# A state-space block and linear attention on one core: the C product moved behind the second scan at slot 10, and half of the gate's Silu read out of PSUM

## The chip, the cores and the metric

The kernel runs on one core of a Trainium2 chip. A core has five engines that run side by side and wait for each other by semaphores: TensorE (PE in the profile) multiplies matrices into PSUM, VectorE (DVE) and GpSimd (POOL) work elementwise, ScalarE (ACT) evaluates functions such as Exp and Silu, and SyncE (SP) issues most of the transfers. Each engine works its own instructions off in order. The metric is the device time of one execution in microseconds; of several executions the median is taken.

## The reference

The input `x` has 4 images of 512 channels with 64 x 64 places, so 4 sequences of 4096 places. Layer 0 takes a group norm, then a layer norm, cuts the channels into 4 chunks of 128 and sends each through a Mamba block. Layer 1 is a linear attention of 8 heads. Each layer is added to its input. Of the Mamba block, what matters here is:

```python
xz = jnp.einsum('bld,ed->ble', x, in_proj_w)
xi, z = jnp.split(xz, 2, axis=-1)
...
xc = jax.nn.silu(xc + conv_b[None, :, None]).transpose(0, 2, 1)
...
def step(h, inp):
    dt_t, B_t, C_t, x_t = inp
    dA = jnp.exp(dt_t[:, :, None] * A)
    h = dA * h + (dt_t * x_t)[:, :, None] * B_t[:, None, :]
    y = jnp.einsum('bds,bs->bd', h, C_t)
    return (h, y)
...
y = ys.transpose(1, 0, 2) + xc * D_param
y = y * jax.nn.silu(z)
return jnp.einsum('bld,od->blo', y, out_proj_w)
```

There are 256 inner channels and 16 states a channel. Two things of this are touched by the change: the product of the state `h` with `C`, and the Silu of `xc` and of the gate `z`.

## The kernel before

**Tiling.** A step is one image, one tile of 512 places and one chunk of 128 channels: 4 x 8 x 4 = 128 steps, the chunk innermost. The 256 inner channels are two halves `e` of 128. For the recurrence, 32 channels with 4 states each fill the 128 partitions; one scan instruction (line 739) runs 512 places of such a row block. A step has 16 slots (line 674) of two scans each, so 32 scans. Slots 0 to 7 belong to half 0, slots 8 to 15 to half 1. Two slots share one `h` buffer (of two, line 733), one row block of `B` and one of `C`.

**A slot** (function `slot`, line 725) issues in this order: GpSimd's product `bx` for the slot after next (`drive`, line 721, three buffers); the loads of later `B` and `C` rows; then twice a scan and, right after it, the Exp that makes the decay for the third scan ahead (`decay`, line 713, three PSUM banks, `LEAD` on line 53). In an even slot the product of the two slots before with `C` comes between the two scans: `product` (line 759) is one VectorE instruction over 4 x 384 places; the last 128 places of each row are multiplied on GpSimd (line 751), with a `C` that a transfer brings (`c_sb`). After `product` comes `fold_states` (line 761), all on TensorE: the next `C` rows into PSUM (line 765, one bank, which the product has to leave first), for the first group of a half the term with `D_param` (the four matmuls of `diagonal`, line 768), and four matmuls that sum over the states into `y` (line 771). The fold is the last reader of `h` and so frees its buffer, which is written again two slots later.

**What is put beside it.** At the end of each slot `after` (line 1108) issues the work of the slot: first what was put off for it (`later`, line 75), then fixed work by slot number, then pieces of norms, projections and attention as TensorE has room for them. The inputs of the step after next are made this way (`inputs`, line 579): at slot 9 the matmul of the gate branch's second half is issued into a bank of a ring of three (`work_bank`, line 67), and at slot 10 the copy out of it (line 608) into `xz`. At slot 10 also stands `silu` (lines 1047 and 1147): one ScalarE instruction over all of `xz`, 4 x 512 places: `xc` of both halves, then `z` of both. Silu and Exp lie in different table sets of ScalarE, so a table load stands before Silu and another after it (line 1149). Slots 3 (softplus, with loads too) and 10 are `AWAY` (line 675); long VectorE instructions of the norms are put there. At slot 9 GpSimd multiplies the gate of half 0 (line 781), and at slot 4 it makes dt times x (line 628). From slot 12 on the matmuls on `xz` for B, C and dt follow (`mixers`, line 642).

The order of all this in the main loop is written by hand; nothing is planned at compile time, and the two steps before the loop run `silu` alone. The lines that set the place of the product are

```python
            if i == 0 and jj == 0 and g:
                product(g - 1)
                fold_states(g - 1, last)
```

where `i` is the scan within the slot and `jj` is 0 in even slots.

Of the kernel before, what the change touches and what calls it, by code (L numbers as in the profile page):

```python
# [10 lines left out]
AF = mybir.ActivationFunctionType  # L11
# [13 lines left out]
def kernel(  # L25
# [24 lines left out]
    nc = tc.nc  # L50
# [4 lines left out]
    NH = DI // P  # L55
# [23 lines left out]
    def work_bank(name, behind=1):  # L79
        held[0] += behind  # L80
        return ps_w.tile([P, T], F32, tag="w", name=name)
# [4 lines left out]
    def later(n, what):  # L86

        done = []

        def both():  # L90
            what()
            done.append(True)

        if now[0] is None:
            both()
        else:
            due.append((now[0] + n, both))
        return done
# [22 lines left out]
    def mm(out_, lhsT, rhs, abreast=1, **how):  # L121

        work["mm"] += (0.25 if rhs.dtype == BF16 else 1.0) * rhs.shape[-1] / T / abreast
        nc.tensor.matmul(out_, lhsT, rhs, **how)  # L124
# [250 lines left out]
    def bc(v, n):  # L375
        return v.unsqueeze(1).to_broadcast([P, n, v.shape[-1]])
# [202 lines left out]
    def inputs(f, xn, c, nm):  # L579

        xz = f["xz"] = wk.tile([P, 2, NH, T], F32, tag="xz", name=f"xz_{nm}", bufs=3)
        pc = [None] * NH

        def taps(e, ks):
            for k in ks:
                mm(
                    pc[e], w_cv[:, k, e * P : (e + 1) * P], xn[:, c, k : k + T],
                    start=(k == 0), stop=(k == NTAP - 1),
                )

        def take(e):
            nc.scalar.activation(xz[:, 0, e, :], pc[e], AF.Identity, bias=cb[:, e : e + 1])

        for e in range(NH):
            pc[e] = work_bank(f"pc_{nm}_{e}", 0)
            taps(e, range(NTAP // 2))
            yield
            taps(e, range(NTAP // 2, NTAP))
            later(1, lambda e=e: take(e))
            yield  # L600
        for e in range(NH):
            pz = work_bank(f"pz_{nm}_{e}", 0)
            mm(
                pz, w_z[:, e * P : (e + 1) * P], xn[:, c, NTAP - 1 : NTAP - 1 + T],
                start=True, stop=True,
            )

            later(1, lambda e=e, pz=pz: nc.scalar.copy(xz[:, 1, e, :], pz))  # L608
            yield

    def time_banks(f, nm):
# [62 lines left out]
    SLOTS = NH * NQ * JJ  # L674
    AWAY = (3, 10)

    def place(g):

        n, r = divmod(g, SLOTS)
        e, r = divmod(r, NQ * JJ)  # L680
        return n, e, *divmod(r, JJ)
# [10 lines left out]
    def b_row(g):  # L692
        n, e, q, _ = place(g)
        b_all[g // JJ] = wk.tile([P, T], F32, tag="b_all", name=f"b_all_{g}", bufs=3)
        for_states(b_all[g // JJ], fs[n]["b_rows"], q)

    def c_tail(g):
        n, e, q, _ = place(g)
        c_sb[g // JJ] = wk.tile([P, T - CUT], F32, tag="c_sb", name=f"c_sb_{g}", bufs=2)
        for_states(c_sb[g // JJ], fs[n]["c_rows"], q)  # L700
# [7 lines left out]
    def decay(k):  # L708

        n, e, q, jj = place(k // 2)  # L710
        j = jj * 2 + k % 2
        dAs[k] = ps_d.tile([P, T], F32, tag="dA", name=f"dA_{k}")
        nc.scalar.activation(  # L713
            dAs[k], fs[n]["d_all", e][:, 0, j, :], AF.Exp, scale=a_t[:, e, j, q : q + 1]
        )

    def drive(g):

        n, e, q, jj = place(g)
        bxs[g] = wk.tile([P, 2, T], F32, tag="bx", name=f"bx_{g}", bufs=3)  # L720
        nc.gpsimd.tensor_tensor(  # L721
            bxs[g], fs[n]["d_all", e][:, 1, jj * 2 : jj * 2 + 2, :], bc(b_all[g // JJ], 2), ALU.mult
        )

    def slot(g, last, after):
        n, e, q, jj = place(g)
        b, t, c = steps[n]
        if g + 2 < last:
            drive(g + 2)
        if jj == 0:  # L730
            if g + 3 * JJ < last:
                b_row(g + 3 * JJ)
            hs[g // JJ] = wk.tile([P, NJ, T], F32, tag="h", name=f"h_{g}", bufs=2)
        elif g + 1 < last:
            c_tail(g + 1)
        h = hs[g // JJ]
        for i in range(2):
            j = jj * 2 + i
            nc.vector.tensor_tensor_scan(  # L739
                h[:, j, :], dAs.pop(2 * g + i), bxs[g][:, i, :],  # L740
                0.0 if t == 0 else st[:, c, e, q, j : j + 1], ALU.mult, ALU.add,
            )
            if 2 * g + i + LEAD < 2 * last:
                decay(2 * g + i + LEAD)
            if i == 0 and jj == 0 and g:
                product(g - 1)
                fold_states(g - 1, last)
        del bxs[g]
        if jj == JJ - 1:
            nc.gpsimd.tensor_copy(st[:, c, e, q, :], h[:, :, T - 1])  # L750
            nc.gpsimd.tensor_tensor(  # L751
                h[:, :, CUT:], h[:, :, CUT:], bc(c_sb.pop(g // JJ), NJ), ALU.mult
            )
        after()

    def product(g):

        own = hs[g // JJ][:, :, :CUT]
        nc.vector.tensor_tensor(own, own, bc(c_all.pop(g // JJ), NJ), ALU.mult)  # L759

    def fold_states(g, last):

        n, e, q, _ = place(g)
        if g + 1 < last:
            c_row(g + 1)
        if q == 0:
            ys[n, e] = ps_y.tile([P, T], F32, tag="y", name=f"y_{n}_{e}")
            diagonal(ys[n, e], dg[:, e, :], fs[n]["xz"][:, 0, e, :])
        h = hs.pop(g // JJ)
        for j in range(NJ):  # L770
            mm(
                ys[n, e][j * BLK : (j + 1) * BLK, :], fold, h[:, j, :],
                start=False, stop=(q == NQ - 1), abreast=NJ,
            )
# [234 lines left out]
    fs = [{} for _ in steps]  # L1009
# [33 lines left out]
    def step_inputs(n):  # L1043
        b, t, c = steps[n]
        return inputs(fs[n], xn[b, t], c, names[n])

    def silu(n):
        nc.scalar.activation(fs[n]["xz"], fs[n]["xz"], AF.Silu)  # L1048

    ahead, late, rest, light = [], [], [], []  # L1050

# [19 lines left out]
    run(tile_norm(0, 0))  # L1071
    run(step_inputs(0))
    silu(0)
    run(mixers(fs[0], names[0]))
    b_row(0)
# [9 lines left out]
    for g in range(2):  # L1085
        drive(g)
    run(step_inputs(1))
    silu(1)
    run(mixers(fs[1], names[1]))
    nc.scalar.preload_act_table_set("natural_log_exp_and_others")  # L1090
# [3 lines left out]
    with tc.manual_schedule():  # L1094
        credit, seen, mix, held[0], held_x[0] = 0.0, work["mm"], iter(()), 0, 0
        for n, (b, t, c) in enumerate(steps):
            f, nm = fs[n], names[n]
# [9 lines left out]
            for s in range(SLOTS):  # L1107
                def after():
# [38 lines left out]
                    if s == 10 and n + 2 < N:  # L1147
                        silu(n + 2)
                        nc.scalar.preload_act_table_set("natural_log_exp_and_others")
# [21 lines left out]
                    seen = work["mm"]  # L1171

                slot(n * SLOTS + s, N * SLOTS, after)
            fs[n - 1].clear() if n else None
        product(N * SLOTS - 1)
# [64 lines left out]
```

## Time and profile before

| | |
|---|---|
| median of 3 runs | 7940.75 us (7933.85 to 7962.12) |
| profiled execution: time | 7963.09 us |
| profiled execution: span of the trace | 7961.4 us |
| granted TensorE clock, mean | 0.897 |
| first to last scan | 122.4 to 7493.4 us |
| product with C (L759) | 1024 times, mean 1726 ns |
| GpSimd's part of it (L751) | 1024 times, mean 1270 ns |
| copy of z out of PSUM (L608) | 256 times, mean 580 ns |
| Silu (L1048) | 128 times, mean 1911 ns |
| each table load | 1283 ns |

How to read the profile: the page of one execution gives each engine's busy time and its share of the span; then groups of equal instructions, with line, engine, operation and what they write and read, count, busy time and mean, and after a second bar the time in which the engine stood idle just before them and who ended most of it. The view of waits has who waited for whom, the total, the number of times and the longest. The timeline has start, length, engine, line, operation and count, and in brackets the idle time before it with its releaser. The profile names only one releaser for a wait that has several.

### The profile page before, as it was taken

The page shows a single profiled execution, that of the slowest core. Times are in us where ns is not written, and L with a number is a line of the kernel's source. Part 1 is how long each engine was busy: PE and PEld are TensorE (multiplying, and loading weights), DVE is VectorE, ACT ScalarE, POOL GpSimd, SP SyncE. Part 2 cuts the span into 40 slices and gives each one's busy share as a digit, 9 for nine tenths or more (in the row PEclk, how much of TensorE's full clock was granted, in tenths as well). Part 3 has the DMA queues.
Part 4 walks back from the last instruction along what each step waited for, and adds up shares of the span by engine and source line. Part 5 has one row for each costly group of instructions (what it writes and reads, how often), then busy time and mean ns, then how long its engine had stood idle before and what let it go on. Part 6 is the DMA issues. An engine that isn't in the chain of part 4 may idle for free.

```text
span 7961.4 us, 90563 instructions
## 1 busy us (share of the span) xinstructions
PE 6453.6 (81%) x24835; PEld 2120.0 (27%) x24880; DVE 6977.7 (88%) x5766; ACT 5507.6 (69%) x8321; POOL 6880.5 (86%) x4597
## 2 busy tenths in 40 slices
PE   5676777677789888888788888898688888888599
PEld 1121212112223222322222223332122332322144
DVE  5999999999999999989999999998999999988600
ACT  4667777777777777767777777677777777777421
POOL 4999999999999899989999899898999999889600
PEclk7888888888899999998899999899899999999799
DMA  5666666666666666777766666677666666676402
GB/s 154 167 168 166 151 155 159 160 155 167 169 179 162 151 163 159 174 189 175 174 155 171 171 157 161 155 185 189 156 167 163 161 161 159 145 194 180 112 32 90
DMA packets 829184, 1265.87 MB, mean 159 GB/s; under 512 B 183912, under 2 KB 317560, under 8 KB 816384
## 3 DMA queue, kind: packets, MB, share of 16 engines
q1 hardware_dynamic: 804736, 1222.32, 61.1%
q0 software_dynamic: 16896, 33.56, 2.4%
q10 hardware_dynamic: 7040, 4.20, 0.2%
q8 instruction: 195, 3.19, 0.2%
q14 instruction: 317, 2.60, 0.1%
HBM read 1052.78 MB, written 206.57 MB: 158 GB/s over the span
## 4 chain that ended last, share of the span: by engine, by line
DVE 33%; PE 21%; ACT 15%; DMA 12%; issue 8%; SPq 6%; POOL 6%; POOLq 0%; ACTq 0%; DVEq 0%
DVE h L739 22%; DVE h L759 9%; DMA d_all<-d_rows 7%; ACT dA L713 5%; PE pq L124 5%; POOL bx L721 4%; PE pc L124 4%; SPq L688 3%; PE y L124 3%; PE pr L124 3%; SPq L639 2%; DMA c_sb<-c_rows 2%; ACT xz L1048 2%; PE po L124 2%; ACT L1048 1%
## 5 line engine op out<-in xcount | busy, mean ns | idle before, releaser
L721 POOL TENSOR_TENSOR bx<-d_all,b_all 128x1024 f32<-128x1024 f32 x2048 | 4824.7, 2367 | 213.3 <-DVE h L739 195.1
L739 DVE TENSOR_TENSOR_SCAN h<-dA,st,bx 128x512 f32<-128x512 f32 x3584 | 4358.9, 1264 | 358.7 <-ACT dA L713 159.0
L713 ACT ACTIVATE dA<-d_all,a_t 128x512 f32<-128x512 f32 x4096 | 2752.9, 687 | 1568.5 <-DVE h L739 1521.8
L759 DVE TENSOR_TENSOR h<-h,c_all 128x1536 f32<-128x1536 f32 x1024 | 1767.5, 1726 | 0.1
L751 POOL TENSOR_TENSOR h<-h,c_sb 128x512 f32<-128x512 f32 x1024 | 1300.2, 1270 | 190.2 <-DMA c_sb<-c_rows 95.2
L124 PE MATMUL y<-h,fold 128*32 128x512 f32 x8192 | 1271.2, 696 | 71.6 <-POOL h L751 67.4
L124 PE MATMUL c_all<-parts,sel 128*128 128x384 bf16 x1024 | 369.9, 361 | 1123.3 <-DVE h L759 1121.7
L124 PE MATMUL pc<-xn,w_cv 128*128 128x512 f32 x2048 | 1045.7, 645 | 122.8 <-DVE xn L414 62.1
L124 PE MATMUL pq<-w_qk,xa 128*128 128x512 f32 x2048 | 965.5, 604 | 7.9 <-issue 5.3
L739 DVE TENSOR_TENSOR_SCAN h<-dA,bx 128x512 f32<-128x512 f32 x512 | 591.2, 1203 | 90.0 <-ACT dA L713 65.1
L124 PEld LDWEIGHTS <-sel 128*128 128x128 bf16 x1280 | 127.1, 99 | 1762.2 <-DVE h L759 1562.5
L124 PEld LDWEIGHTS pc<-xn,w_cv 128*128 128x128 f32 x2048 | 389.5, 201 | 747.1 <-issue 424.7
L124 PEld LDWEIGHTS pq<-w_qk,xa 128*128 128x128 f32 x2048 | 398.6, 196 | 439.6 <-issue 422.4
L124 PE MATMUL pr<-xb,m 128*128 128x512 f32 x1024 | 485.3, 612 | 7.5 <-DMA xb<-x 3.6
L124 PE MATMUL pp<-xn,w_pr 128*128 128x512 f32 x1024 | 477.7, 597 | 4.8 <-DVE xn L414 4.8
L124 PEld LDWEIGHTS y<-h,fold 128*32 128x32 f32 x8192 | 170.6, 114 | 644.0 <-issue 344.9
L124 PE MATMUL y<-xz,dg 32*32 32x512 f32 x2048 | 337.3, 734 | 0.0
L781 POOL TENSOR_TENSOR xz<-xz 128x512 f32<-128x512 f32 x256 | 325.7, 1272 | 9.2 <-ACT xz L778 9.2
L832 ACT ACTIVATE kq<-pq 128x512 f32<-128x512 f32 x256 | 150.5, 588 | 259.9 <-PE pq L124 259.2
L124 PE MATMUL pd<-xz,w_xp 128*128 128x512 f32 x512 | 323.4, 764 | 7.8 <-ACT xz L1048 7.8
L628 POOL TENSOR_TENSOR dt<-dt,xz 128x1024 f32<-128x1024 f32 x128 | 302.3, 2361 | 24.7 <-ACT dt L620 24.6
L124 PE MATMUL pz<-xn,w_z 128*128 128x512 f32 x512 | 275.4, 631 | 11.7 <-ACT xz L608 8.2
(179 smaller groups left out, 6034.1 us busy)
## 6 DMA issues: line engine op xcount, KB each, us to landing
d_all<-d_rows SPq DMA_DIRECT2D x2048, 256.0 KB, 6.7
b_all<-b_rows SPq DMA_DIRECT2D x4096, 64.0 KB, 2.2
d_rows<-dt SPq DMA_DIRECT2D x256, 512.0 KB, 3.6
c_sb<-c_rows SPq DMA_DIRECT2D x4096, 16.0 KB, 1.8
xs<-in_x_dram SPq DMA_DIRECT2D x32, 1024.0 KB, 6.3
xn<-in_x_dram SPq DMA_DIRECT2D x32, 1024.0 KB, 6.2
xr<-in_x_dram POOLq DMA_DIRECT2D x32, 1024.0 KB, 10.7
x<-xr SPq DMA_DIRECT2D x32, 1024.0 KB, 4.2
```

What stands on the lines that cost most here:

```text
L124: nc.tensor.matmul(out_, lhsT, rhs, **how)
L628: nc.gpsimd.tensor_tensor(f["both"][:, 1], f["both"][:, 0], f["xz"][:, 0], ALU.mult)
L639: nc.sync.dma_start(d[k * BLK : (k + 1) * BLK, v], src)
L688: nc.sync.dma_start(dst[k * BLK : (k + 1) * BLK, :], rows_[q * KS + k, :].partition_broadcast(BLK))
L713: nc.scalar.activation(dAs[k], fs[n]["d_all", e][:, 0, j, :], AF.Exp, scale=a_t[:, e, j, q : q + 1])
L721: nc.gpsimd.tensor_tensor(bxs[g], fs[n]["d_all", e][:, 1, jj * 2 : jj * 2 + 2, :], bc(b_all[g // JJ], 2), ALU.mult)
L739: nc.vector.tensor_tensor_scan(h[:, j, :], dAs.pop(2 * g + i), bxs[g][:, i, :], 0.0 if t == 0 else st[:, c, e, q, j : j + 1], ALU.mult, AL ...
L751: nc.gpsimd.tensor_tensor(h[:, :, CUT:], h[:, :, CUT:], bc(c_sb.pop(g // JJ), NJ), ALU.mult)
L759: nc.vector.tensor_tensor(own, own, bc(c_all.pop(g // JJ), NJ), ALU.mult)
L781: nc.gpsimd.tensor_tensor(f["xz"][:, 1, e, :], f["xz"][:, 1, e, :], f["xz"][:, 0, e, :], ALU.mult)
L832: nc.scalar.activation(qk[i], pq, AF.Relu)
L1048: nc.scalar.activation(fs[n]["xz"], fs[n]["xz"], AF.Silu)
```

## The change

Two edits. In a slot 10 (the slot whose number in its step is `AWAY[1]`) `product` and `fold_states` are issued after the second scan and its decay, not after the first; in the other even slots they stay. And the gate branch's second half is no longer copied into `xz`: the bank is kept in `f["pz"]`, and `silu` becomes two instructions, one over the first 3 x 512 places of `xz` in place, one that reads the bank and writes the last 512.

```diff
@@ -605,7 +605,9 @@
-            later(1, lambda e=e, pz=pz: nc.scalar.copy(xz[:, 1, e, :], pz))
+            if e + 1 < NH:
+                later(1, lambda e=e, pz=pz: nc.scalar.copy(xz[:, 1, e, :], pz))
+            f["pz"] = pz
             yield
@@ -742,7 +744,7 @@
-            if i == 0 and jj == 0 and g:
+            if i == int(g % SLOTS == AWAY[1]) and jj == 0 and g:
                 product(g - 1)
                 fold_states(g - 1, last)
@@ -1045,7 +1047,9 @@
     def silu(n):
-        nc.scalar.activation(fs[n]["xz"], fs[n]["xz"], AF.Silu)
+        xz = fs[n]["xz"].rearrange("p i e t -> p (i e) t")
+        nc.scalar.activation(xz[:, : 2 * NH - 1], xz[:, : 2 * NH - 1], AF.Silu)
+        nc.scalar.activation(xz[:, 2 * NH - 1], fs[n]["pz"], AF.Silu)
```

## The prediction, made before the result was known

> **What bounds the kernel now.** First the page: busy shares and the costliest groups.
>
> ```profile
> PE 6453.6 (81%) x24835; PEld 2120.0 (27%) x24880; DVE 6977.7 (88%) x5766; ACT 5507.6 (69%) x8321; POOL 6880.5 (86%) x4597
> L721 POOL TENSOR_TENSOR bx<-d_all,b_all 128x1024 f32<-128x1024 f32 x2048 | 4824.7, 2367 | 213.3 <-DVE h L739 195.1
> L739 DVE TENSOR_TENSOR_SCAN h<-dA,st,bx 128x512 f32<-128x512 f32 x3584 | 4358.9, 1264 | 358.7 <-ACT dA L713 159.0
> ```
>
> VectorE and GpSimd are nearly equal and feed each other: the scan (L739) needs `bx`, and the drive (L721) needs a `bx` buffer that a scan has emptied. A microsecond taken from one counts only as far as the other follows. Next, whom VectorE waits for:
>
> ```profile
> DVE h L739 <- ACT dA L713: 224.0, 186, 46.4
> DVE h L739 <- PE y L124: 90.8, 88, 3.9
> DVE h L739 <- POOL bx L721: 78.0, 70, 4.7
> ```
>
> I then counted the scans (two a slot, 32 a step), which gives each its slot. I use 125 of the 128 steps: the first and the last two differ. The slot-12 second scan (the 26th of a step) waits for its decay (L713) in 82 of them, 65.2 us in all. The other large place is slot 5, 80.0 us, after the softplus tables; the change doesn't touch it. Of the 125, 57 have no other VectorE work between slots 10 and 11; most others have a long instruction there (1.3 or 2.3 us), which covers part of the delay. Now one step by the timeline; slot 10 begins at 881.58. VectorE and ScalarE:
>
> ```profile
> 882.76 1.73 DVE L759 TENSOR_TENSOR h<-h,c_all 128x1536 f32<-128x1536 f32 x1
> 884.40 4.80 DVE L739 TENSOR_TENSOR_SCAN h<-dA,st,bx 128x512 f32<-128x512 f32 x4
> 889.12 1.72 DVE L759 TENSOR_TENSOR h<-h,c_all 128x1536 f32<-128x1536 f32 x1
> 892.66 2.46 DVE L739 TENSOR_TENSOR_SCAN h<-dA,st,bx 128x512 f32<-128x512 f32 x2 [1.81 <-ACT dA L713]
> ```
> ```profile
> 885.71 0.69 ACT L713 ACTIVATE dA<-d_all,a_t 128x512 f32<-128x512 f32 x1 [1.68 <-DVE h L739]
> 886.34 0.58 ACT L608 COPY xz<-pz 128x512 f32<-128x512 f32 x1
> 886.82 0.58 ACT L391 COPY got_var_b<-var_sums_b 128x512 f32<-128x512 f32 x1
> 887.42 1.28 ACT L1048 ACT_TABLE_LOAD   x1
> 888.71 1.91 ACT L1048 ACTIVATE xz<-xz 128x2048 f32<-128x2048 f32 x1
> 890.64 1.28 ACT L1149 ACT_TABLE_LOAD   x1
> 891.93 2.73 ACT L713 ACTIVATE dA<-d_all,a_t 128x512 f32<-128x512 f32 x4
> ```
>
> Read it as a loop: the decay at 885.71 waited 1.68 us for slot 10's second scan, which stood behind the product at 882.76. Only then could the copy, a table load, Silu and the load back begin, and only after these the decay that the scan at 892.66 awaits. TensorE and GpSimd, the same step and, last, a later step's slot 10:
>
> ```profile
> 884.54 0.34 PE L124 MATMUL c_all<-parts,sel 128*128 128x384 bf16 x1 [1.37 <-DVE h L759]
> 884.81 1.06 PE L124 MATMUL y<-xz,dg 32*32 32x512 f32 x8
> 885.80 1.06 PE L124 MATMUL y<-h,fold 128*32 128x512 f32 x8
> ...
> 894.02 2.34 POOL L721 TENSOR_TENSOR bx<-d_all,b_all 128x1024 f32<-128x1024 f32 x1 [0.57 <-DVE h L739]
> ...
> 996.05 0.34 PE L124 MATMUL c_all<-parts,sel 128*128 128x384 bf16 x1 [3.04 <-DVE h L759]
> 996.32 1.90 PE L124 MATMUL y<-xz,dg 32*32 32x512 f32 x8
> ```
>
> The first says that the fold waits for the product, the second that GpSimd loses only 0.57 of the 1.81 us, the last that TensorE runs slower after a long wait (1.90 against 1.06).
>
> **What the Trainium skill says.** "ScalarE: Activation LUTs", What ACT_TABLE_LOAD costs: about 1283 ns a load, 0.833 ns an element, neighbours overlapping by some 93 ns; the trace has 1283, and 1911 ns for 2048 elements. "Perfetto Trace Analysis", Optimizing Scalar/DVE Operations: ScalarE's access overhead is smaller in PSUM than in SBUF; the trace agrees weakly (Relu out of PSUM 588 ns, Square out of SBUF 614). "TensorE: Matmul & The Clock Gate", What's actually happening: an idle window of some 3.4 us halves the clock; here a wait of 3.04 us was enough.
>
> **Part 1, Silu out of PSUM.** Gone: 126 copies in the loop (L608, 580 ns each). They save about 0.52 us each on ScalarE, the start-to-start distance without the overlap. Silu becomes two instructions: 1911 − 512 × 0.833 = 1484 ns (estimate) and one of 512 out of PSUM, for which I take the Relu's 588. Less 93 of overlap that is 1979, 0.07 more than now. Both use one table set, so no load is added. Net 0.45 us sooner, bounds 0.3 (no overlap) and 0.55. The PSUM bank is given back only after the second Silu, not before the table load: some 3.3 us later in ScalarE's order, and 1.7 later in time where Part 2 brings the rest 1.65 sooner. The ring has three banks, so the third later allocation would wait; with at most two queued banks in use, that is work of slot 11 or 12, which TensorE reaches after slot 10's folds. Taken as nothing; if uncovered, 1.7 us in the some 15 steps in which TensorE waits for L608 now, 25 us of TensorE time.
>
> **Part 2, the product behind the second scan.** VectorE's sum is unchanged. The scan ends 1.65 us sooner (the product less its overlap), and so may the following decay and the table chain behind it, no further than that decay's present idle time. That is over 1.5 us in 51 steps and under 0.5 in 57: there ScalarE was itself late, mostly behind a copy waiting for TensorE. The product ends 1.2 us later. With it go, on TensorE, the C row's matmul, the gate's diagonal and the fold, and all queued behind them; on GpSimd and the DMA queues nothing is moved. TensorE stood ready in 48 steps and moves by 1.2 us there; in 56 it comes over 1.2 us after the product and doesn't notice; the rest shift partly.
>
> The fold frees the `h` buffer which slot 12 writes. In the step shown it ends at 886.86 and would end at 888.04; the scan needs it at 887.95 (three scans before the product at 889.12). Adding the 0.17 us that such a release takes in other steps gives 0.25 us of new wait. Over all steps these waits add 10 us, in 18 steps.
>
> **The sum.** Step by step, the stall of 65.2 us shrinks by the smaller of itself and (idle before the decay, at most 1.65) + 0.45: that removes 46 us. 28 of them are in 32 steps where the decay now idles long, 18 in 49 where it doesn't. Less the 10 us of new fold waits: 36 us sooner on VectorE. What GpSimd can pass on is limited to its own waits for VectorE from slot 12 to slot 8 of the next step; taking the smaller of the two in each step leaves 25.6 us. The rest is eaten by GpSimd's unbroken row of drives. So 7963.09 (the profiled execution) − 25.6 = 7937.5. That execution lies 22.3 us above the median of the runs, 7940.75; from there I forecast 7915. What is late next is GpSimd's drive at slot 12 or 0, the `c_sb` transfer that the gate waits for (95.2 us in all now), and the fold.
>
> **Rivals.**
> - *The forecast* (0.46): 12 to 39 us less.
> - *All of it passes through* (0.26): the slot-12 wait disappears, GpSimd's 66 us of waiting before its drive at slot 13 with it, and shorter steps feed themselves: 45 to 70 less, about 7883. For it: those two sums match. Against: in half the steps ScalarE was late already.
> - *Hidden anyway* (0.14): the scan only waits for someone else, the fold on a slow TensorE. In seven steps that wait is 3.0 us already and will be over 4; a cold fold ends some 4.2 us after the product, not 2.4, and cancels what such a step gains. No change within 12 us: 7941.
> - *Slower* (0.14): TensorE loses time at slot 10. In 48 steps it stands 1.2 us longer, 58 us, plus half a cold group (0.9 us) in some 16 of them, 14 us. If it can't catch up before slot 8, the folds come late there and the 72 us show: 7941 − 25 + 72 = 7988. Against: the windows view of the loop (120 to 7490) gives TensorE 5966 us busy of 7370, so 1404 us idle, 11 us a step. It decides only from the point where less than 1.2 us of a step's idle time lies after slot 10.
>
> **How the numbers follow.** About 0.5%, 40 us, is what this measurement can tell from no change. Forecast and hidden lie inside, the second rival outside; the slower one lies outside in 0.11 and inside in 0.03. With a little of the forecast's edge beyond 40 us, faster is 0.29, same 0.60, slower 0.11. The range goes from 7872 (all of it) to 7970 (part of the slower case); the likeliest alone is 7902 to 7929.
>
> **What would show it.** In the trace after: 126 fewer copies at L608; two Silu of about 1484 and 588 ns with one load before them; the slot-12 wait for L713 falling from 65 to about 20 us or less; waits of the scan for `y` up by about 10; GpSimd's waits for L739 down by some 25, and its `c_sb` waits up. I am wrong if the slot-12 wait stays (ScalarE was bound elsewhere), if it goes and the span doesn't (GpSimd or DMA bound), or if waits for `y` at slots 8 to 12 rise by more than 40.

## The result, and the profile after

The changed kernel takes 7927.6 us (median of 11 runs, 7918.6 to 7935.39) against 7954.56 us of the kernel before (11 runs). The ratio is 0.9969, with a 95% interval of 0.9960 to 0.9978: some 25 us less (0.0031 × 7954.56). The 7940.75 us shown above are the median of three of these runs of before; the forecast of 25.6 us less than the median is to be held against the ratio, and not the 7915 us that followed from the lower median. (Three line numbers in the description above were off: `LEAD`, `work_bank` and `later` stand on lines 67, 79 and 86.) In the changed kernel the line of the scan is 741, that of the decay 715, of the product 761, of the drive 723; the two Silu are 1051 and 1052.

The page of the kernel after, busy shares and groups:

```profile
PE 6453.3 (81%) x24837; PEld 2103.7 (27%) x24880; DVE 6974.9 (88%) x5766; ACT 5453.7 (69%) x8321; POOL 6880.3 (87%) x4597
L723 POOL TENSOR_TENSOR bx<-d_all,b_all 128x1024 f32<-128x1024 f32 x2048 | 4826.0, 2368 | 170.3 <-DVE h L741 154.9
L741 DVE TENSOR_TENSOR_SCAN h<-dA,st,bx 128x512 f32<-128x512 f32 x3584 | 4354.8, 1264 | 336.1 <-ACT dA L715 120.0
L124 PE MATMUL y<-xz,dg 32*32 32x512 f32 x2048 | 363.1, 787 | 0.0
```

ScalarE has 54 us less to do, as the durations say: 128 × (580 + 1911 − 1484 − 579) ns = 55 us. The other engines have what they had, but the D term's matmuls, 734 ns in the mean before, now take 787. The waits of VectorE, after:

```profile
DVE h L741 <- ACT dA L715: 174.6, 127, 44.5
DVE h L741 <- PE y L124: 92.1, 97, 4.0
DVE h L741 <- POOL bx L723: 74.5, 61, 4.8
```

The wait for decays fell by 49 us; that for `y` looks unchanged, but at the first scan of slot 12 most of the waits named after other engines end within 0.3 us of a fold's end too. So I count by place, over all 128 steps: each scan by its number in the step, with all idle time ahead of it over 60 ns. The slot-12 second scan waits 15.4 us in all instead of 65.2. The first scan of the same slot waits 69.4 instead of 47.2. And the second scan of slot 10, which never waited, now waits 8.3 us in 14 steps for its decay: the product used to stand before it and gave ScalarE time. GpSimd's idle time before its drive at slot 13 fell by 28 us, from 73.6 to 45.8 (the prediction had 66 for the first).

The step that the prediction showed is the best picture of how a stall moves. VectorE and ScalarE, the same step, after; slot 10 begins at 883.08:

```profile
882.95 0.72 ACT L473 ACTIVATE sq_b<-xn,about 128x512 f32<-128x512 f32 x1
883.58 1.29 ACT L715 ACTIVATE dA<-d_all,a_t 128x512 f32<-128x512 f32 x2
884.80 0.58 ACT L609 COPY xz<-pz 128x512 f32<-128x512 f32 x1
885.28 1.30 ACT L715 ACTIVATE dA<-d_all,a_t 128x512 f32<-128x512 f32 x2
886.51 0.58 ACT L391 COPY got_var_b<-var_sums_b 128x512 f32<-128x512 f32 x1
887.11 1.28 ACT L1051 ACT_TABLE_LOAD   x1
888.41 1.48 ACT L1051 ACTIVATE xz<-xz 128x1536 f32<-128x1536 f32 x1
889.80 0.58 ACT L1052 ACTIVATE xz<-pz 128x512 f32<-128x512 f32 x1
890.40 1.28 ACT L1153 ACT_TABLE_LOAD   x1
```
```profile
885.49 1.73 DVE L761 TENSOR_TENSOR h<-h,c_all 128x1536 f32<-128x1536 f32 x1
887.14 2.45 DVE L741 TENSOR_TENSOR_SCAN h<-dA,st,bx 128x512 f32<-128x512 f32 x2
891.31 1.28 DVE L741 TENSOR_TENSOR_SCAN h<-dA,st,bx 128x512 f32<-128x512 f32 x1 [1.72 <-PE y L124]
892.51 1.73 DVE L761 TENSOR_TENSOR h<-h,c_all 128x1536 f32<-128x1536 f32 x1
```
```profile
887.28 0.34 PE L124 MATMUL c_all<-parts,sel 128*128 128x384 bf16 x1 [1.98 <-DVE h L761]
887.54 1.67 PE L124 MATMUL y<-xz,dg 32*32 32x512 f32 x8
889.14 1.94 PE L124 MATMUL y<-h,fold 128*32 128x512 f32 x8
```

The decay no longer waits, the table chain is done 1.7 us earlier in the step (its second load ends 8.6 us after the slot's first scan began; before it was 10.34), and the second scan's wait of 1.81 us is gone. But TensorE, which now waited 1.98 us for the product and not 1.37, runs the D term and the fold at little more than half speed: together they took 2.05 us before and 3.5 now. (Each has four matmuls, and each of these has two records, so x8.) The fold ends 8.0 us after the slot's first scan began; before it was 5.3. It frees `h` late, and the first scan of slot 12 waits 1.72 us. In this step the change moves the stall by one scan and gains next to nothing.

### The profile page after: what moved, and what is told of

Same layout as the page of the kernel before. It is cut to its first block, busy times and chain, and to the rows that moved or that the text cites. A ratio compares the mean times of both kernels' runs of the same rounds, so it can differ in the third digit from the quotient of the medians.

```text
span 7927.9 us, 90689 instructions
## 1 busy us (share of the span) xinstructions
PE 6453.3 (81%) x24837; PEld 2103.7 (27%) x24880; DVE 6974.9 (88%) x5766; ACT 5453.7 (69%) x8321; POOL 6880.3 (87%) x4597
## 4 chain that ended last, share of the span: by engine, by line
DVE 33%; PE 27%; ACT 11%; DMA 10%; issue 8%; POOL 6%; SPq 4%; POOLq 0%; DVEq 0%; ACTq 0%
DVE h L741 21%; DVE h L761 9%; PE y L124 5%; PE pc L124 5%; DMA d_all<-d_rows 5%; PE pq L124 5%; POOL bx L723 4%; ACT dA L715 4%; SPq L690 3%; PE pr L124 3%; PE po L124 2%; PE pp L124 2%; DMA c_sb<-c_rows 2%; SPq L641 1%; DMA b_all<-b_rows 1%
## 5 line engine op out<-in xcount | busy, mean ns | idle before, releaser
L723 POOL TENSOR_TENSOR bx<-d_all,b_all 128x1024 f32<-128x1024 f32 x2048 | 4826.0, 2368 | 170.3 <-DVE h L741 154.9
L753 POOL TENSOR_TENSOR h<-h,c_sb 128x512 f32<-128x512 f32 x1024 | 1300.9, 1270 | 208.8 <-DMA c_sb<-c_rows 115.7
L124 PE MATMUL y<-xz,dg 32*32 32x512 f32 x2048 | 363.1, 787 | 0.0
```

Source lines behind the costliest of these rows:

```text
L723: nc.gpsimd.tensor_tensor(bxs[g], fs[n]["d_all", e][:, 1, jj * 2 : jj * 2 + 2, :], bc(b_all[g // JJ], 2), ALU.mult)
L753: nc.gpsimd.tensor_tensor(h[:, :, CUT:], h[:, :, CUT:], bc(c_sb.pop(g // JJ), NJ), ALU.mult)
```

## The experiments

All ratios are against the kernel before, run on the same chip. "First" and "second" are the waits ahead of the two scans of slot 12, summed over the profiled execution; "slow" is the number of steps, of 125, in which the group of TensorE at slot 10 from the C row to the fold's end takes over 2.5 us (2.3 is usual).

```
run                                          ratio (95%)              first  second  slow
before (the profile shown first)             1                         47.2    65.2    15
the change, first measurement                0.9969 (0.9960-0.9978)    69.4    15.4    40
after_again                                  0.9970 (0.9961-0.9980)    70.2    15.4    39
e1_product_alone                             0.9990 (0.9983-0.9997)    73.5    22.0    37
e2_silu_alone                                0.9964 (0.9952-0.9977)    48.0    37.4    12
e3_diagonal_ahead                            0.9957 (0.9944-0.9971)    45.4    17.0     -
e4_before_light_pool                         0.9996 (0.9989-1.0002)    41.7    71.9    16
e5_after_light_pool                          0.9967 (0.9954-0.9979)    68.8    15.4    34
e6_silu_diagonal_ahead                       0.9964 (0.9950-0.9978)    49.6    39.6     -
e7_both_gates_psum                           1.0037 (1.0025-1.0050)   138.8    33.2    23
e8_diagonal_twice                            1.0020 (1.0013-1.0026)   107.3    19.8    15
e9_diagonal_ahead_again                      0.9963 (0.9951-0.9976)    44.6    17.3     -
e10_silu_diagonal_again                      0.9977 (0.9967-0.9987)    49.1    39.0     -
e11_silu_alone_again                         0.9970 (0.9963-0.9977)    46.2    39.0    11
```

(Where the D term is issued ahead, the group is shorter by it and isn't counted.)

**Each part by itself.** Four kernels on one chip. First the change again, then the product's move without the Silu edit:

```diff
-            if i == 0 and jj == 0 and g:
+            if i == int(g % SLOTS == AWAY[1]) and jj == 0 and g:
```

and the Silu edit alone, which is the change with this line put back.

> The change as it is, beside its parts on one chip. Both theories: ratio 0.997, waits of the slot-12 scans as in the trace after: about 69 us before the first (for y mostly), about 15 before the second (for dA).

> Only the product is moved at slot 10, copy and single Silu as before. Theory A (each step's table chain starts sooner by no more than the idle time of the decay ahead of it; the late fold takes part of that back): the slot-12 second scan's wait falls from 65 by 37 to about 28 us, the first scan's rises by some 20, so little is left: ratio 0.998 to 1.000. Rival B (the move is the change, the copy next to nothing): ratio 0.997 or lower, as with both.

> Only Silu reads the gate's second half out of PSUM; the product stays behind the first scan. Theory A: every table chain is 0.45 us shorter, the slot-12 second scan's wait falls by 27 to about 38 us, the fold is where it was, so nothing is taken back: ratio 0.997 to 0.998. Rival B: within 5 us of before, ratio 0.9993 to 1.0005. If the longer held PSUM bank costs TensorE time, its waits for the two Silu show it and the ratio is over 1.000.

Silu alone brings all of the change's gain, in both of its runs (7925.8 and 7926.9 us; the change 7927.6 and 7931.3); the move alone brings 8 us (its interval allows 2 to 14) and, on top of Silu, nothing that can be measured. Theory A's waits came out near what was written: 22.0 against 28 for the move, 37.4 against 38 for Silu, whose ratio lies a little under the 0.997 to 0.998 expected. Rival B falls. The waits add up: the move takes 43.2 us from the second scan of slot 12, but puts 26.3 on the first and 8.1 on the second scan of slot 10, which leaves 8.8; Silu takes 27.8 and puts 0.8 on the first scan, which leaves 27, and 28 were measured. VectorE's waits with the move alone, then with Silu alone, show the exchange, decays against `y`:

```profile
DVE h L739 <- ACT dA L713: 180.1, 134, 46.5
DVE h L739 <- PE y L124: 103.1, 104, 3.2
```
```profile
DVE h L741 <- ACT dA L715: 187.8, 139, 44.5
DVE h L741 <- PE y L124: 81.5, 81, 5.3
```

The longer held bank costs nothing that shows: in the whole run with Silu alone TensorE waited for the second Silu twice, 1.0 us together.

**The fold shortened.** The D term needs only `xz` and the bank of `y`, so in a slot 10 it can go ahead of the product:

```diff
+            if i == 0 and g % SLOTS == AWAY[1]:
+                open_y(n, e)
             if i == int(g % SLOTS == AWAY[1]) and jj == 0 and g:
...
+    def open_y(n, e):
+        ys[n, e] = ps_y.tile([P, T], F32, tag="y", name=f"y_{n}_{e}")
+        diagonal(ys[n, e], dg[:, e, :], fs[n]["xz"][:, 0, e, :])
...
-        if q == 0:
+        if q == 0 and (n, e) not in ys:
```

> The change, with the four matmuls of the D term at slot 10 issued ahead of the product (they don't need it). Theory A (part of the gain goes back because the fold ends late and TensorE is slowed by its longer wait): the fold ends about 1.0 us sooner, slow groups at slot 10 get fewer than 40, the slot-12 first scan's wait falls from 69 to about 45 us, ratio 0.994 to 0.996. Rival C (what VectorE gains beyond this GpSimd and the transfers eat anyway): the wait falls, the ratio stays 0.997.

The first scan's wait went to 45.4 us, as expected, and the time to 7918 us, 13 less than the change on the same chip (the intervals still overlap). TensorE in the same step as above, slot 10 beginning at 875.36:

```profile
877.51 1.06 PE L124 MATMUL y<-xz,dg 32*32 32x512 f32 x8
879.55 0.32 PE L124 MATMUL c_all<-parts,sel 128*128 128x384 bf16 x1 [0.98 <-DVE h L763]
879.80 1.07 PE L124 MATMUL y<-h,fold 128*32 128x512 f32 x8
```

The D term fills the wait, the rest of it is short, and the fold runs at full speed: it ends 5.5 us after the slot's first scan began, against 8.0 with the change.

**Is it GpSimd that eats the rest?** The prediction said so. The gate's product of half 0 at slot 9 is left out in the kernel before and in the changed one, so that this half of `y` isn't gated:

```diff
                     if s == 9:
-                        gate(f, 0)
                         if nxt is not None:
```

> The kernel before without GpSimd's gate product of half 0 at slot 9 (that half is left ungated): 1.27 us less GpSimd work a step, 163 us in all. If GpSimd's row of drives limits, some 60 to 130 us come out: ratio 0.984 to 0.993. If it doesn't: ratio over 0.996. The slot-12 second scan waits as before, about 65 us.

> The change with the same gate product left out. Theory A (GpSimd keeps some 10 of 36 us of the change's gain): against the kernel before without that product the ratio is 0.9955 or lower, so the change is worth 36 us or more once GpSimd has room. Theory D (GpSimd keeps nothing; the gain is small because the late fold and new waits take back about 30 of 50 us): it is worth 20 to 27 us here too, the quotient of the two ratios 0.997.

Taking work off GpSimd doesn't change the time measurably (0.9989 to 1.0002), though it is busy for 86% of the span. The page of the kernel before without that gate, then GpSimd's waits there:

```profile
PE 6456.6 (81%) x24835; PEld 2117.2 (27%) x24880; DVE 6975.5 (88%) x5766; ACT 5506.3 (69%) x8321; POOL 6728.2 (85%) x4469
```
```profile
POOL bx L721 <- DVE h L739: 267.3, 361, 6.6
POOL h L751 <- DMA c_sb<-c_rows: 120.1, 70, 6.6
POOL st L750 <- DVE h L739: 118.0, 100, 5.4
```

It does 152 us less, and its waits for VectorE grow by 72 before the drive (195.1 before) and 39 before the state's copy (78.9 before). The idle time before the drive at slot 13, inside the stretch in which the prediction had GpSimd without room, grew from 73.6 to 125.1 us. And with this room the change is worth no more: 0.9967 / 0.9996 = 0.9971. Theory D, that GpSimd keeps nothing of it, fits; the 36 us of Theory A don't. But the two intervals leave some 12 to 34 us (an estimate), so that GpSimd keeps a few us isn't excluded, and work was taken off at this one place of the loop alone.

**The D term ahead without the move, and both gates out of PSUM.** The first has the Silu edit, issues `open_y` at the start of slot 10 and leaves the product where it was; in the second neither half of the gate is copied, and `silu` reads both banks, ahead of `xc` (its edit, against the kernel before):

```diff
-            if e + 1 < NH:
-                later(1, lambda e=e, pz=pz: nc.scalar.copy(xz[:, 1, e, :], pz))
-            f["pz"] = pz
+            f["pz", e] = pz
...
+        for e in range(NH):
+            nc.scalar.activation(xz[:, 1, e], fs[n]["pz", e], AF.Silu)
+        nc.scalar.activation(xz[:, 0], xz[:, 0], AF.Silu)
```

> Silu out of PSUM, the D term's matmuls at slot 10 issued at the slot's start, the product in its old place. Theory A and D: the slot-12 first scan's wait falls from 48 to 30 to 40 us (the fold ends up to 1 us sooner where TensorE was ready), the second's stays at 37: 0.9955 to 0.9965. If moving the product is worth something once the fold is short, this one lies 5 us or more above the change with the D term ahead (7918 us), at 7923 or more; if not, it is as fast.

> Silu reads both halves of the gate branch out of PSUM, the product in its old place: the other 126 copies go too, but two of the ring's three banks are held until Silu. If a held bank costs nothing: the slot-12 second scan's wait falls from 37 to about 30 us, ratio 0.995 to 0.996. If it costs TensorE time: its waits for the Silu are tens of us, the scan's waits for y rise by more than 20 us, ratio over 0.998.

The first missed its expectation for the wait: 49.6, not 30 to 40. With the product in its old place TensorE comes to it late for its own work in most steps: in 94 of the 125 it took up the C row without a wait for the product (77 in the kernel before). The second answers what one bank more costs. The second scan's wait fell by 4 us (7 were hoped for), but with two of three banks held TensorE waits for the Silu, and VectorE waits longer for TensorE. Who waited for these banks to be read, then VectorE's waits:

```profile
  PEld var_sums_b L124: 24.4, 5
  PE var_sums_b L124: 20.3, 5
  PE pq L124: 9.7, 6
```
```profile
DVE h L739 <- PE y L124: 164.2, 103, 8.4
DVE h L739 <- ACT dA L713: 139.7, 130, 3.6
```

The first scan of slot 12 alone waits 138.8 us, 91 more than with one bank held, and the kernel is slower than before. The waits of matmuls that are named after these Silu come to 35 us, in 15 waits (the weight loads show the same waits again); that the rest of the 91 has the banks behind it too is likely and not shown.

**Late or slow?** To tell the fold's late start from TensorE's slow clock, the D term is issued twice in the changed kernel: ahead of the product into the bank of `y`, where it is overwritten, and again in its place.

> The change, with the four matmuls of the D term issued twice at slot 10: once ahead of the product, whose result is thrown away, and once in its old place. TensorE works in its wait, but the fold ends as late as in the change. If the slow TensorE makes the fold late: slow groups fall from 40 to under 15 and the slot-12 first scan's wait from 70 to some 55 us or less. If the order does it: the wait stays at 65 to 75 us though slow groups get fewer, and the ratio stays near 0.997.

Neither outcome came: slow groups fell to 15, but the first scan's wait rose to 107 us. The second D term also adds 1 us of work where TensorE was late anyway, and there an extra microsecond ahead of the fold is dear: 7969 us, 0.5% over the change. To compare like with like I sort the steps: 73 in which TensorE stood ready for the product in both runs of the change, 37 of them slow. The first scan's wait in these 37: 4.1 us before, 24.3 with the change, 24.6 with the move alone, 16.4 with the D term twice (whose group takes 2.74 us there in the mean; 3.76 with the change, 2.85 before), 2.3 with the D term ahead. In the other 36 ready steps it is 1.9 before and 3.7 after, in the remaining 52 it is 39.4 and 37.2. So all of the rise stands in the 37 steps in which TensorE is slow. Of 20 us there, some 8 go when the speed is restored, and the late start has the other 12, as far as this sorting can part them: the kernel with two D terms is slower elsewhere.

**Once more on one chip.** 

> The change with the D term ahead, again, beside the two without the product's move on one chip. If the move is worth something once the fold is short: 5 to 12 us under the one with the D term ahead and the product in its old place; if not, within 4 us of it.

> Silu out of PSUM and the D term ahead, product in its old place, again: ratio 0.9955 to 0.997, within 5 us of Silu out of PSUM alone.

> Silu out of PSUM alone, again, on the chip of the three others: ratio 0.996 to 0.9975, the slot-12 second scan's wait at 37 us as in the first run.

The D term ahead with the move: 7919 us; without the move 7931, a ratio over the 0.9955 to 0.997 expected; Silu alone 7927. The order of the medians is the same as before. The move is worth some 12 us once the fold is short, about what the waits say: 39.0 − 17.3 at the second scan less 8.3 at slot 10 makes 13 (the first scan's 49.1 − 44.6 would add 4.5). The intervals of the three overlap, so this is likely and not settled. The version with the move and the D term ahead has the lowest median in both of its runs (0.9957 and 0.9963).

## Why the prediction was right, and where it wasn't

- *The time.* Forecast 25.6 us less, measured 25 by the ratio. The likeliest case came, inside its own range of 12 to 39.
- *Part 1.* The sizes hold: 1484 ns and 579 for the two Silu (1484 and 588 taken), one load, and the net gain of 0.45 us is what makes the wait of 38 us expected for Silu alone come out at 37.4. That the held bank costs nothing holds for one bank; with two held the kernel is some 30 us slower than before (1.0037).
- *Part 2, the stall removed.* 46 us expected from the idle times ahead of the decay, 49.8 measured.
- *Part 2, the fold.* Mis-sized: 10 us in 18 steps, measured 22.2 in all. I let the fold keep its present speed and only start later, which has about the 12 us of the sorted steps. That the longer wait itself slows TensorE stood only under the rivals, with some 16 steps at risk; the slow groups rose by 25. Left out was also the cover that the product gave the second scan of slot 10, 8.3 us. (In the working, the scan that needs `h` at 887.95 is the last one before the product at 889.12, not three before it; the time is right. And Part 1's lower bound without overlap comes to 0.36 us, not 0.3; neither bears on the sum.)
- *The share that GpSimd keeps.* This step failed, as far as the runs can tell. I cut 36 us to 25.6, because GpSimd's row of drives has hardly a gap, and took its busy share for a limit. With 152 us of its work gone the time stayed where it was, and the change was worth no more.
- *So the sum was right by luck.* The two places with new waits took 30 us and not 10. Against these 20 stand three errors the other way: GpSimd took none that shows, and not 10; the stall gave 4 more; and other slots gave some 8 that nobody had forecast. What is left at slots 10 and 12, 49.8 − 22.2 − 8.3 = 19, and these 8 us make the 27 us by which all scan waits fell (400.8 to 373.6, without the wait ahead of the first scan of all); the time fell by 25. This sum itself is loose: another profile of the changed kernel gave 377.7, two of Silu alone 371.1 and 383.6, two of the D term ahead 350.4 and 370.5. The waits at single places repeat much better: with the change, 69.4 and 70.2 us at the first scan of slot 12 and 15.4 twice at the second.
- *The signs.* Of those named, the copies, the two Silu and the slot-12 wait came. GpSimd's waits for the scan fell by 40 us, not 25 (195.1 to 154.9), and its waits for `c_sb` rose, from 95.2 to 115.7. The wait for `y` by name rose by 1 us and not 10; the 22 us showed only by place.
- *The rivals.* All passing through (45 to 70) didn't come, since the waits arose elsewhere. "Hidden anyway" named the mechanism that took part of the gain, the fold on a slow TensorE, and had too few steps for it (seven; the slow groups rose by 25), but that was not enough to hide the gain. The slower case didn't come: outside the first scan of slot 12 the waits of the scans for `y` didn't rise (67.8 us before, 58.4 after).
- *What the prediction didn't ask:* which of the two parts pays. One of them alone, the Silu edit, has the whole measured gain.

## What to carry to other kernels

When a change joins two edits that shorten the same wait, price each one alone with all that it moves: the cheap one may have all of the gain, and the other may pay with a new wait for what it saves. A busy share near 90% doesn't make an engine the limit: ask what happens to its waits if its work is taken away, or try it. Before an instruction is put later, look at who runs behind it on the engine that waits for it, put what doesn't need it ahead, and see whether the longer pause costs that engine speed.

## What the runs showed of the hardware

TensorE slowed down after shorter waits than I had thought of. "TensorE: Matmul & The Clock Gate", What's actually happening, in the Trainium skill tells of an idle window of some 3.4 us, placed freely in time; in the step shown a single wait of 1.98 us was followed by a group at 1.67 and 1.94 us where 1.06 is full speed. The trace has the granted clock on record, in stretches of 3.41 us or multiples of it. The two stretches of this step, with TensorE's busy time and matmul records, the clock, and the share and rate of the DMA engines:

```profile
884.46:887.87 3.41, 1.43 (x9) 1.00 1.07 214
887.87:891.28 3.41, 3.21 (x16) 0.50 1.08 208
```

So the slow group ran at half the clock, and the stretch before it was not idle: TensorE was busy for 1.43 of its 3.41 us. I counted this over the whole trace of the kernel before, by the records that it has. A stretch at full clock in which TensorE was busy under 40% was followed by one at half clock all 153 times, one busy for 60% or more only 6 times of 1545. Once at half clock, a stretch busy under 70% was followed by another at half clock all 192 times. So the stretch need not be idle, as the skill has it: by this count what matters here is how full it is, and a wait of 2 us can be enough.
